# Block 1's router: the first of the largest logits found for four tiles at once

## The chip, the cores and the metric

The program runs on one core of one Trainium2 chip. All data are float32. The metric is the device time of one execution in microseconds; of several executions the median counts. The core has five engines with an instruction queue each: PE (TensorE), DVE (VectorE), ACT (ScalarE), POOL (GpSimd) and SP (SyncE, which here only issues DMAs). An engine works through its queue in order, so whatever waits holds up all that stands behind it in that queue.

## The reference

The input x has 32 sequences of 256 tokens with 128 features, 8192 tokens in all. Two blocks follow each other; each computes `x + s * silu(m)` from the layer-normalized x, where s is an attention branch and m a mixture-of-experts branch. Block 0 has two layers of softmax attention and 64 experts with eight choices per token; block 1 has linear attention and 32 experts with one choice per token. The change is in block 1's router. What it must compute, shortened:

```python
logits = x @ gate_w                        # [8192, 32]
topk_ids = jnp.argmax(logits, axis=-1)     # the first of the largest
topk_val = jnp.max(logits, axis=-1)
scores = jax.nn.sigmoid(topk_val)[:, None]
xs = x * scores
tokens_per_expert = jnp.zeros((E,), jnp.int32).at[topk_ids].add(1)
order = jnp.argsort(topk_ids)
sorted_x = xs[order]                       # rows grouped by expert, then three grouped matmuls
```

## The kernel before

A tile is 128 tokens, one per partition; a group is four tiles (512 tokens), and there are 16 groups. The kernel is written as generators that yield between steps; `run` and `rolling` interleave them. A scheduler then fixes the order of each engine's queue from the dependencies and its own estimate of times, and semaphores are set for what remains. A change in a few instructions can therefore move others on every queue.

The stages, in the order of time: block 0's attention, router and experts (to about 757 us, with the last layers' matmuls L663 and L681 reaching to 849 us); block 1's routing, interleaved with that tail and then alone (757 to 942 us); linear attention together with the scattering of rows to experts' slots (L860, 64 scatters issued by POOL, 942 to 1047 us); linear attention with the routed experts (L972, L982, L987); and the last sums.

Per group, `route` does the following, and the prediction's lines are these:

- It loads the two halves of block 0's expert sums and x by SP (L185, L187, L189), adds the halves on POOL (L188), and makes the gate on ACT and DVE (L192 to L198; the first eight groups by Tanh, the others by Silu).
- It normalizes the rows: statistics on DVE (L109, L110), four small operations on POOL (L111 to L120), the normalized rows `c_xn` on ACT (L122), four transposes on PE (L132), a copy to SBUF (L204).
- It multiplies by the router's weights (L208): four matmuls into one PSUM bank of 32 logits per tile. There are two such banks ("mm"), shared with L235, L265, L663, L681 and others.
- DVE takes, tile by tile, the eight largest logits (L216) and their places (L217, two instructions: a load of the eight values and a search); it casts the first places to float (L219) and compares the experts' numbers with them, which gives the one-hot rows `hot` (L221).
- ACT and DVE make the score from the largest logit (L223, L225); POOL scales the normalized rows with it into `s_rows` (L227).
- Running counts give each row its rank within its expert: sums on DVE (L231, L233), three matmuls (L235, L236, L239), and the rank on DVE (L240, L242, L243).

`shared1` is the shared expert of the same group: gate and up matmuls (L253, L254), activation (L256 to L260), down matmuls (L265). For groups 0 to 5 it is done later, beside the linear attention.

The work tiles come from two pools: `first_work` has one buffer per name and serves groups 0 to 3, and of the later groups those whose number is divisible by three; `mid_work` has two and serves the others. `c_xn` is such a tile, so in the small pool the next group's L122 waits until L227 of the group before has read the old rows.

When all groups are routed, the counts of all groups give the slots (`dest`, L854), and only then can the first scatter (L860) start.

Of the kernel before, what the change touches and what calls it, by code (L numbers as in the profile page):

```python
# [16 lines left out]
F32 = mybir.dt.float32  # L17
I32 = mybir.dt.int32
U32 = mybir.dt.uint32
AF = mybir.ActivationFunctionType  # L20
ALU = mybir.AluOpType
AX = mybir.AxisListType
# [3 lines left out]
P = 128  # L26
# [3 lines left out]
GT = 4  # L30
# [4 lines left out]
E1, F1 = 32, 256  # L35
# [25 lines left out]
def recurrent_kernel(ctx: ExitStack, tc: tile.TileContext, x, consts, small0, wsd, wgu, wd, small1, bias1, wr, out):  # L61
    nc = tc.nc
    vec, act, pool, pe, sp = nc.vector, nc.scalar, nc.gpsimd, nc.tensor, nc.sync

    def bcast(ap, axis, n):
        ap = ap.unsqueeze(axis)
        return ap.broadcast_to([n if i == axis else s for i, s in enumerate(ap.shape)])
# [5 lines left out]
    def bank(tag="mm", bufs=2):  # L73
        return psum.tile([P, GW], F32, tag=tag, name=f"ps_{tag}", bufs=bufs)
# [9 lines left out]
    def rows(ap, g):  # L84
        return ap[g * GW : (g + 1) * GW].rearrange("(t p) d -> p t d", p=P)
# [8 lines left out]
    def const(name):  # L94
        return con[:, cc[name][0] : cc[name][1]]
# [7 lines left out]
    def normed(wk, src, dst, on=pool):  # L103

        st = wk.tile([P, GT, 6], F32, name="bn_st")
        mv = wk.tile([P, GT, 2], F32, name="bn_mv", bufs=3)
        rs = wk.tile([P, 2, GT], F32, name="bn_rs", bufs=3)
        for j in range(GT):
            vec.bn_stats(st[:, j], src[:, j])  # L109
            vec.bn_aggr(mv[:, j], st[:, j])  # L110
        pool.tensor_scalar(rs[:, 0], mv[:, :, 1], 1.0, EPS, ALU.mult, ALU.add)  # L111
        pool.tensor_tensor(rs[:, 0], rs[:, 0], power, ALU.pow)  # L112
        if on is vec:
            ins = pool.tensor_tensor(rs[:, 1], mv[:, :, 0], rs[:, 0], ALU.mult)
            for j in range(GT):
                vec.tensor_scalar(dst[:, j], src[:, j], rs[:, 0, j : j + 1], rs[:, 1, j : j + 1], ALU.mult, ALU.subtract)
            return ins
        pool.tensor_scalar(rs[:, 1], mv[:, :, 0], -1.0, 0.0, ALU.mult, ALU.add)
        if on is act:
            pool.tensor_tensor(rs[:, 1], rs[:, 1], rs[:, 0], ALU.mult)  # L120
            for j in range(GT):
                ins = act.activation(dst[:, j], src[:, j], AF.Identity, scale=rs[:, 0, j : j + 1], bias=rs[:, 1, j : j + 1])  # L122
            return ins
        for j in range(GT):
            ins = pool.tensor_scalar(dst[:, j], src[:, j], rs[:, 1, j : j + 1], rs[:, 0, j : j + 1], ALU.add, ALU.mult)  # L125
        return ins

    def transposed(src):

        ps = bank("tr", 2)  # L130
        for j in range(GT):
            pe.transpose(ps[:, j * P : (j + 1) * P], src[:, j], ident)  # L132
        return ps
# [11 lines left out]
    at1, x_at, xt_at, hots = {}, {}, {}, {}  # L145

    def par1(name, at=0, n=None):
        a, b = s1[name]
        t, a, b = (at1["sw_c"], a - cut, b - cut) if a >= cut else (at1["sw_a"], a, b)
        return t[:, a + at : b if n is None else a + at + n]  # L150

    def room(pool_, gs):
        for g in gs:
            x_at[g] = pool_.tile([P, GT, D], F32, name=f"x_{g}")
            xt_at[g] = pool_.tile([P, GW], F32, name=f"xt_{g}")
            if g % 4 == 0:
                hots[g // 4] = pool_.tile([P, NT // 4, E1], F32, name=f"hot_{g // 4}")

    def hot_of(g):
        return hots[g // 4][:, g % 4 * GT : (g % 4 + 1) * GT]  # L160

    def begin1(pool_):
        t = at1["sw_c"] = pool_.tile([P, n_s1 - cut], F32, name="sw_c")
        sp.dma_start(t, small1[:, cut:])
        at1["rank"] = pool_.tile([P, NT], F32, name="rank")
        at1["before"] = pool_.tile([P, NG + 1, E1], F32, name="before")
        vec.memset(at1["before"][:, 0], 0.0)
        at1["ones"] = pool_.tile([P, P], F32, name="ones")
        vec.memset(at1["ones"], 1.0)
        at1["eiota"] = pool_.tile([P, E1], F32, name="eiota")  # L170
        pool.iota(at1["eiota"], [[1, E1]], base=0, channel_multiplier=0, allow_small_or_imprecise_dtypes=True)
        room(pool_, range(EARLY))

    works = []
# [1 line left out]
    def work(n):  # L176

        return works[len(works) > 1 and n % 3 > 0]

    def route(g):  # L180

        wk = works[0] if g < EARLY else work(g)
        tl = slice(g * GT, (g + 1) * GT)
        gr = wk.tile([P, GT, D], F32, tag="gate", name="c_g")
        sp.dma_start(gr, rows(moe0[0], g))  # L185
        more = wk.tile([P, GT, D], F32, tag="chan", name="c_m")
        sp.dma_start(more, rows(moe0[1], g))  # L187
        pool.tensor_tensor(gr, gr, more, ALU.add)  # L188
        sp.dma_start(x_at[g], rows(x, g))  # L189
        if g < TANH:  # L190

            act.activation(more, gr, AF.Tanh, scale=0.5)  # L192
            vec.scalar_tensor_tensor(gr, more, 1.0, gr, ALU.add, ALU.mult)
            vec.scalar_tensor_tensor(gr, gr, 0.5, s_all[:, tl], ALU.mult, ALU.mult)
        else:
            act.activation(gr, gr, AF.Silu)
            vec.tensor_tensor(gr, gr, s_all[:, tl], ALU.mult)
        vec.tensor_tensor(x_at[g], x_at[g], gr, ALU.add)  # L198
        yield
        xn = wk.tile([P, GT, D], F32, tag="tok", name="c_xn")  # L200
        normed(wk, x_at[g], xn, act)
        yield
        ps = transposed(xn)
        act.copy(xt_at[g], ps)  # L204
        yield
        lp = bank()
        for j in range(GT):
            pe.matmul(  # L208
                lp[:, j * E1 : (j + 1) * E1], xt_at[g][:, j * P : (j + 1) * P], par1("router"),
                start=True, stop=True,  # L210
            )
        lg = lp[:, : GT * E1].rearrange("p (t e) -> p t e", e=E1)
        m8 = wk.tile([P, GT, 8], F32, name="c_m8")
        i8 = wk.tile([P, GT, 8], U32, name="c_i8")
        for j in range(GT):
            vec.max(m8[:, j], lg[:, j])  # L216
            vec.max_index(i8[:, j], m8[:, j], lg[:, j])  # L217
        fi = wk.tile([P, GT], F32, name="c_fi")
        vec.tensor_copy(fi, i8[:, :, 0])  # L219
        hot = hot_of(g)  # L220
        vec.tensor_tensor(hot, bcast(at1["eiota"], 1, GT), bcast(fi, 2, E1), ALU.is_equal)  # L221
        score = wk.tile([P, GT], F32, name="c_sc")
        act.activation(score, m8[:, :, 0], AF.Tanh, scale=0.5)  # L223
        yield
        vec.tensor_scalar(score, score, 0.5, 0.5, ALU.mult, ALU.add)  # L225
        for j in range(GT):
            pool.tensor_scalar(s_all[:, g * GT + j], xn[:, j], score[:, j : j + 1], 0.0, ALU.mult, ALU.add)  # L227


        cum = wk.tile([P, GT, E1], F32, name="c_cum")  # L230
        vec.tensor_copy(cum[:, 0], hot[:, 0])  # L231
        for j in range(1, GT):
            vec.tensor_tensor(cum[:, j], cum[:, j - 1], hot[:, j], ALU.add)  # L233
        ps = bank()
        pe.matmul(ps[:, : GT * E1], const("tri"), hot.rearrange("p t e -> p (t e)"), start=True, stop=False)  # L235
        pe.matmul(  # L236
            ps[:, E1 : GT * E1], at1["ones"], cum[:, : GT - 1].rearrange("p t e -> p (t e)"), start=False, stop=True,
        )
        pe.matmul(ps[:, GT * E1 : (GT + 1) * E1], at1["ones"], cum[:, GT - 1], start=True, stop=True)  # L239
        vec.tensor_tensor(at1["before"][:, g + 1], at1["before"][:, g], ps[:, GT * E1 : (GT + 1) * E1], ALU.add)  # L240
        pos = wk.tile([P, GT, E1], F32, name="c_pos")
        vec.tensor_tensor(pos, ps[:, : GT * E1].rearrange("p (t e) -> p t e", e=E1), hot, ALU.mult)  # L242
        vec.tensor_reduce(at1["rank"][:, tl], pos, AX.X, ALU.add)  # L243
        yield
# [58 lines left out]
    def begin(g):  # L303
        yield from route(g)
        if g >= INL:
            yield from shared1(g)


    with ExitStack() as c0:
# [3 lines left out]
        wk = c0.enter_context(tc.tile_pool(name="wk0", bufs=2, side="right"))  # L313
# [489 lines left out]
    wk = ctx.enter_context(tc.tile_pool(name="wk1", bufs=2))  # L803
# [334 lines left out]
```

## Time and profile before

| | |
|---|---|
| median of three runs | 1338.09 us (1333.77 to 1339.4) |
| the profiled execution, whole | 1336.66 us |
| its span, first to last instruction | 1334.9 us |
| mean granted TensorE clock | 0.972 |
| busy: PE, PEld, DVE, ACT, POOL | 1222.2, 863.2, 943.5, 787.6, 650.6 us |
| 757 to 942 us (routing): PE, DVE, ACT, POOL busy | 156.5, 130.7, 94.3, 84.1 of 185 us |
| router on DVE: L216, L217, L219, L221 busy | 11.8, 17.3, 2.6, 4.9 us |

The span is divided by engine: an engine's busy time is the sum of its instructions' times, without waits. The granted clock is the share of full speed that TensorE was allowed[...]. A line such as "L227 <- DVE c_sc L225" in a list of waits means that the instruction of line 227 stood idle until the instruction of line 225 on DVE, which wrote c_sc, was done. In the groups of instructions the two numbers after the bar are the group's busy time and the mean time of one instruction in nanoseconds. A float32 matmul appears as two records, so "x2" of a 128x512 matmul is one instruction of the program.

### The profile page before, as it was taken

What the parts mean: (1) busy time and instruction counts of PE and PEld (TensorE: products, weight loads), DVE (VectorE), ACT (ScalarE), POOL (GpSimd) and SP (SyncE); (2) the same over time, 40 slices, a digit from 0 to 9 for tenths busy, and PEclk for the clock granted to TensorE, in tenths of its full rate; (3) what the DMA queues carried; (4) which work ended last, traced back from release to release, by engine and by line L of the source; (5) the groups of instructions that cost most, each with busy time, mean ns of one, the idle gap of its engine ahead of it and who ended that gap; (6) DMA issues with size and microseconds to landing.
All of it is one profiled execution on the core that took longest, in us unless ns stands there. A gap on an engine that the chain in (4) does not pass through costs nothing. (4 is left out here: it accounts for less than half of the span.)

```text
span 1334.9 us, 22827 instructions
## 1 busy us (share of the span) xinstructions
PE 1222.2 (92%) x7425; PEld 863.2 (65%) x7425; DVE 943.5 (71%) x3064; ACT 787.6 (59%) x1858; POOL 650.6 (49%) x1020
## 2 busy tenths in 40 slices
PE   6989999999999899999998877889999899999997
PEld 4546576566566476667666545566566688888873
DVE  4699779879879856656655766776878666676537
ACT  1786666676676567676765766444545465564543
POOL 6362822733722557656644456252477434444540
PEclk9999999999999999999999998989989899999999
DMA  6020301311211332132211133311311366767767
GB/s 183 22 56 25 112 24 48 113 31 41 96 33 40 112 76 59 34 84 56 65 20 34 36 99 94 93 49 40 113 42 45 101 206 199 220 200 220 225 218 207
DMA packets 135078, 125.80 MB, mean 94 GB/s; under 512 B 17104, under 2 KB 110256, under 8 KB 134832
## 3 DMA queue, kind: packets, MB, share of 16 engines
q1 hardware_dynamic: 123696, 108.57, 27.4%
q0 software_dynamic: 11264, 15.78, 4.9%
q8 instruction: 59, 0.97, 0.3%
q14 instruction: 59, 0.48, 0.1%
HBM read 83.63 MB, written 40.68 MB: 93 GB/s over the span
## 5 line engine op out<-in xcount | busy, mean ns | idle before, releaser
L601 ACT ACTIVATE a_pr<-ps_sc,a_nm 128x256 f32<-128x256 f32 x256 | 119.4, 480 | 58.9 <-DVE a_nm L592 58.8
L987 POOL DMA_INDIRECT back<-e_ys,e_toi x96 | 95.1, 991 | 106.3 <-ACT e_ys L986 73.2
L111 POOL TENSOR_SCALAR bn_rs<-bn_mv 128x4 f32<-128x4 f32 x112 | 27.9, 249 | 230.4 <-DVE bn_mv L110 207.0
L663 PE MATMUL ps_mm<-xt,sw 128*128 128x512 f32 x256 | 135.4, 636 | 1.6 <-ACT e_y L523 0.9
L125 POOL TENSOR_SCALAR z<-s_rows,bn_rs 128x128 f32<-128x128 f32 x256 | 129.3, 526 | 6.6
L681 PE MATMUL ps_mm<-sw,m_h 128*128 128x128 f32 x1024 | 128.3, 280 | 2.2 <-ACT e_y L523 1.3
L681 PEld LDWEIGHTS ps_mm<-sw,m_h 128*128 128x128 f32 x1024 | 119.9, 193 | 12.7 <-issue 6.0
L668 DVE SCALAR_TENSOR_TENSOR m_h<-m_h,m_z 128x512 f32<-128x512 f32 x128 | 90.4, 710 | 46.4 <-ACT m_h L667 45.9
L112 POOL TENSOR_TENSOR bn_rs<-bn_rs,power 128x4 f32<-128x4 f32 x112 | 117.4, 1048 | 1.2
L665 ACT ACTIVATE m_z<-ps_mm,fold 128x512 f32<-128x512 f32 x128 | 87.4, 686 | 30.2 <-PE ps_mm L663 29.9
L592 DVE TENSOR_REDUCE a_nm<-ps_sc 128x2 f32<-128x512 f32 x128 | 83.3, 679 | 30.6 <-PE ps_sc L586 30.5
L972 PE MATMUL ps_sc<-e_xt,e_w 128*128 128x128 f32 x768 | 100.8, 278 | 1.0 <-ACT e_xt L1009 0.6
L972 PEld LDWEIGHTS ps_sc<-e_xt,e_w 128*128 128x128 f32 x768 | 94.5, 194 | 9.8 <-issue 7.8
L586 PE MATMUL ps_sc<-a_qk,a_qk 64*128 64x256 f32 x512 | 96.4, 411 | 1.2 <-ACT a_pr L601 1.1
L524 POOL DMA_INDIRECT sums<-e_y,sidx x32 | 51.1, 1598 | 80.4 <-ACT e_y L523 42.7
L618 PE MATMUL ps_tr<-con,a_pr 128*128 128x128 f32 x512 | 76.2, 279 | 9.5 <-ACT a_pt L619 5.6
L618 PEld LDWEIGHTS ps_tr<-con,a_pr 128*128 128x128 f32 x512 | 59.5, 144 | 38.3 <-issue 20.2
L667 ACT ACTIVATE m_h<-m_z 128x512 f32<-128x512 f32 x128 | 80.8, 635 | 1.7
L860 POOL DMA_INDIRECT xslot<-s_rows,dest x64 | 68.4, 1069 | 24.1 <-issue 18.5
L619 ACT COPY a_pt<-ps_tr 128x512 f32<-128x512 f32 x128 | 71.9, 591 | 12.4 <-PE ps_tr L618 11.4
L558 PE MATMUL ps_mm<-xt,sw 128*128 128x512 f32 x128 | 70.3, 657 | 6.4 <-ACT xt L546 3.0
L627 PE MATMUL ps_mm<-a_pt,a_v 128*64 128x256 f32 x512 | 70.9, 396 | 4.2 <-ACT m_z L665 3.6
(236 smaller groups left out, 2950.4 us busy)
## 6 DMA issues: line engine op xcount, KB each, us to landing
e_w<-in_wr_dram SPq DMA_DIRECT2D x96, 384.0 KB, 4.0
xslot<-zero SPq DMA_DIRECT2D x4, 1548.0 KB, 6.7
e_x<-xslot SPq DMA_DIRECT2D x24, 258.0 KB, 3.6
e_wg<-in_wgu_dram SPq DMA_DIRECT2D x16, 384.0 KB, 3.2
x_in<-in_x_dram SPq DMA_DIRECT2D x16, 256.0 KB, 3.2
tab<-s_rows SPq DMA_DIRECT2D x16, 256.0 KB, 2.4
sums<-s_y SPq DMA_DIRECT2D x16, 256.0 KB, 2.3
sums<-zero SPq DMA_DIRECT2D x4, 1024.0 KB, 8.4
```

The lines of the kernel that those rows point to most:

```text
L112: pool.tensor_tensor(rs[:, 0], rs[:, 0], power, ALU.pow)
L125: ins = pool.tensor_scalar(dst[:, j], src[:, j], rs[:, 1, j : j + 1], rs[:, 0, j : j + 1], ALU.add, ALU.mult)
L586: pe.matmul(sc[h][:, j * SEQ : (j + 1) * SEQ], qk[0][hd, q0 : q0 + P], qk[1][hd, b * SEQ : (b + 1) * SEQ], start=True, stop=True,)
L592: vec.tensor_reduce(nm[:, 2 * h : 2 * h + 2], sc[h].rearrange("p (j k) -> p j k", k=SEQ), AX.X, ALU.max, negate=True)
L601: act.activation(pr[:, n], sc[h][:, j * SEQ : (j + 1) * SEQ], AF.Exp, bias=nm[:, n : n + 1], accum_out=su[:, n : n + 1],)
L618: pe.transpose(pts[:, n * P : (n + 1) * P], pr[:, n, k * P : (k + 1) * P], ident)
L663: pe.matmul(ps, par("w1", l * FF0 + f * P, P), xt, start=True, stop=True)
L665: act.activation(z, ps, AF.Identity, bias=fold[:, l, 3 + f : 4 + f])
L668: vec.scalar_tensor_tensor(h, h, 1.0, z, ALU.add, ALU.mult)
L681: pe.matmul(ps[:, j * D : (j + 1) * D], hs[f][:, j * P : (j + 1) * P], par("w2", l * FF0 + f * D, D), start=f == 0, stop=f == 3,)
L972: pe.matmul(ps[:, c * P : (c + 1) * P], wt[:, c * P : (c + 1) * P], xt, start=True, stop=True)
L987: ins = pool.indirect_dma_start(out=back, out_offset=bass.IndirectOffsetOnAxis(ap=to, axis=0), in_=ys, in_offset=None,)
```

## The change

The eight largest logits and their places are no longer sought. One reduction over all four tiles gives the largest logit of each token. The logits are compared with it, which marks every expert that has it; the marks are multiplied by the experts' numbers, which now run from 32 down to 1, so that the largest number among the marked is the first expert; a second reduction finds that number; and the comparison with the experts' numbers gives the one-hot rows as before. The score reads the first reduction's result. The tile `c_top` has three buffers in either pool. The lines of the kernel behind the router move by one.

```diff
         at1["eiota"] = pool_.tile([P, E1], F32, name="eiota")
-        pool.iota(at1["eiota"], [[1, E1]], base=0, channel_multiplier=0, allow_small_or_imprecise_dtypes=True)
+        pool.iota(at1["eiota"], [[-1, E1]], base=E1, channel_multiplier=0, allow_small_or_imprecise_dtypes=True)
...
         lg = lp[:, : GT * E1].rearrange("p (t e) -> p t e", e=E1)
-        m8 = wk.tile([P, GT, 8], F32, name="c_m8")
-        i8 = wk.tile([P, GT, 8], U32, name="c_i8")
-        for j in range(GT):
-            vec.max(m8[:, j], lg[:, j])
-            vec.max_index(i8[:, j], m8[:, j], lg[:, j])
-        fi = wk.tile([P, GT], F32, name="c_fi")
-        vec.tensor_copy(fi, i8[:, :, 0])
+        top = wk.tile([P, GT], F32, name="c_top", bufs=3)
+        vec.tensor_reduce(top, lg, AX.X, ALU.max)
         hot = hot_of(g)
-        vec.tensor_tensor(hot, bcast(at1["eiota"], 1, GT), bcast(fi, 2, E1), ALU.is_equal)
+        vec.tensor_tensor(hot, lg, bcast(top, 2, E1), ALU.is_equal)
+        vec.tensor_tensor(hot, hot, bcast(at1["eiota"], 1, GT), ALU.mult)
+        which = wk.tile([P, GT], F32, name="c_fi")
+        vec.tensor_reduce(which, hot, AX.X, ALU.max)
+        vec.tensor_tensor(hot, bcast(at1["eiota"], 1, GT), bcast(which, 2, E1), ALU.is_equal)
         score = wk.tile([P, GT], F32, name="c_sc")
-        act.activation(score, m8[:, :, 0], AF.Tanh, scale=0.5)
+        act.activation(score, top, AF.Tanh, scale=0.5)
```

## The prediction

> **What bounds the kernel now.** I read the page first (PE is busy 92% of the span, DVE 71%, ACT 59%, POOL 49%), then cut the span into stages, because the change touches one stage only: the routing of block 1, from the first router matmul at 757 us to the first scatter at 942 us. The stage table is the view that matters; its columns are length, busy time of PE, PEld, DVE, ACT and POOL with instruction counts, granted TensorE clock, DMA share and GB/s.
>
> ```profile
> 757.00:796.00 39.00, 34.25 (x212) 22.86 (x211) 29.37 (x110) 27.19 (x70) 19.38 (x34) 1.00 0.30 82
> 796.00:850.00 54.00, 40.15 (x230) 30.75 (x231) 35.81 (x149) 29.48 (x60) 27.80 (x45) 0.84 0.24 69
> 850.00:900.00 50.00, 41.63 (x181) 27.27 (x181) 36.41 (x205) 20.61 (x47) 26.19 (x48) 0.86 0.34 94
> 900.00:942.00 42.00, 40.49 (x240) 29.68 (x239) 29.09 (x148) 17.01 (x37) 10.72 (x29) 1.00 0.13 38
> ```
>
> In the last row PE is the bound (40.5 of 42 us). In the second and third it is not: PE idles 13.9 and 8.4 us there, and what it does runs at a granted clock of 0.84 and 0.86. No single engine is full; a chain that goes round all of them is the limit. The waits of 755 to 950 us name it (who waits, for what; total us, times, longest):
>
> ```profile
> POOL s_rows L227 <- DVE c_sc L225: 31.9, 8, 8.0
> ACT c_xn L122 <- POOL s_rows L227: 23.8, 11, 3.5
> ...
> PE ps_tr L132 <- ACT c_xn L122: 10.4, 6, 6.8
> ...
> PE ps_mm L235 <- DVE bn_mv L110: 4.2, 1, 4.2
> ...
> PE ps_mm L235 <- DVE hot L221: 2.0, 1, 2.0
> ```
>
> Read upwards from PE: it waits for normalized rows, these wait for POOL's scaling of the group before (the small work pool has one buffer of c_xn, so a new one cannot be written until the old one is scaled), and the scaling waits for the score c_sc. The fourth line says bn_mv, but the matmul's own input is hot; bn_mv merely ended last. In the timeline the worst turn of this ring looks so (start, length, engine, line; the bracket is the idle time before):
>
> ```profile
> 794.62 0.17 DVE L216 MAX8 c_m<-ps_mm 128x8 f32<-128x32 f32 x1
> 797.47 1.08 DVE L193 SCALAR_TENSOR_TENSOR c_g<-c_m,c_g 128x512 f32<-128x512 f32 x1 [2.67 <-ACT c_m L192]
> ...
> 798.64 0.14 DVE L225 TENSOR_SCALAR c_sc<-c_sc 128x4 f32<-128x4 f32 x1
> ...
> 798.89 3.22 POOL L227 TENSOR_SCALAR s_rows<-c_xn,c_sc 128x128 f32<-128x128 f32 x4 [0.90 <-DVE c_sc L225]
> ...
> 802.14 1.65 ACT L122 ACTIVATE c_xn<-x,bn_rs 128x128 f32<-128x128 f32 x4 [3.49 <-POOL s_rows L227]
> ...
> 802.69 0.86 PE L132 MATMUL ps_tr<-con,c_xn 128*128 128x128 f32 x2 [6.76 <-ACT c_xn L122]
> ```
>
> The logits were there at 792.3. The score is made from the fourth MAX8, and in DVE's fixed order the score's last step stood behind an unrelated gate operation (L193) that waited for ACT. PE stood for 6.8 us.
>
> **What the change removes and adds, per group of four tiles (16 groups).** The prices come from the groups by line and shape (busy us, mean ns):
>
> ```profile
> L217 DVE FIND_INDEX8 c_i<-c_m,ps_mm 128x8 uint32<-128x32 f32 x64 | 12.0, 188 | 0.0
> L216 DVE MAX8 c_m<-ps_mm 128x8 f32<-128x32 f32 x64 | 11.8, 184 | 18.5 <-PE ps_mm L208 18.4
> ...
> L217 DVE MATCH_VALUE_LOAD c_i<-c_m,ps_mm 128x8 f32 x64 | 5.3, 83 | 0.8
> ...
> L221 DVE TENSOR_TENSOR hot<-eiota,c_fi 128x128 f32<-128x128 f32 x16 | 4.9, 308 | 0.2
> ...
> L242 DVE TENSOR_TENSOR c_pos<-ps_mm,hot 128x128 f32<-128x128 f32 x16 | 4.5, 282 | 0.0
> L243 DVE TENSOR_REDUCE rank<-c_pos 128x4 f32<-128x128 f32 x16 | 4.4, 276 | 0.2
> ...
> L219 DVE CAST c_fi<-c_i 128x4 f32<-128x4 uint32 x16 | 2.6, 161 | 0.1
> ```
>
> - Removed: 4 x (184 + 83 + 188) + 161 = 1.98 us in 13 instructions. L221 stays.
> - Added: two reductions of 128x128 to 128x4 (276 each, the row of L243), one comparison with the logits in PSUM (282, L242: also one PSUM and one SBUF input), one product of two SBUF tiles (308, L221). Sum 1.14 us in 4 instructions. Reading PSUM in the first reduction is not shown at this size: L393 reduces 128x256 from PSUM in 419 ns, so 128 elements cannot cost more than that; I take 276 and keep 419 for the range (+2.3 us in all, on DVE).
> - Net: -0.84 us of DVE a group, -13.4 us over the stage. DVE is 70% busy there, so this is not the gain; it counts only where PE waits for DVE.
> - The reversed experts' numbers cost nothing: one iota of the same shape on POOL. No DMA is added, and none is meant to move.
>
> Three latencies change, and these count more than busy time. (1) The score needed the fourth MAX8, the tenth instruction of the old chain counting the loads, with other DVE work between the links; now it needs the first reduction. (2) The hot rows needed 14 instructions, now 5. With nothing between, 903.50 to 905.73 us is 2.2 us; five dependent operations at 0.28 us plus 0.03 us each (the step from hot to the next in that stretch) are 1.5 us. With fills between, I read from the end of L208 to the end of L221 8.1, 3.4, 5.4 and 6.3 us for the second to the fifth group. (3) The PSUM bank of the logits (two of this kind, which L663, L681, L235 and L265 share) is freed after the second instruction instead of after the last FIND_INDEX8.
>
> **Where PE gets it back**, each against the profiled execution (span 1334.9 us, whole 1336.7):
> - 796 to 802.7: in the built order the score's step on DVE now precedes L193, and on POOL one c_g addition precedes the scaling instead of two. POOL ends its norm at 795.5, + 1.27 (one L188) + 1.5 to 2.4 (four L227) + 0.5 (first c_xn): PE resumes at 799.3 to 799.7 instead of 802.7. Gain 3 us.
> - 821.0 to 825.2: hot came 5.4 us after its logits. In the new order seven short operations (statistics and the score) remain between the five links: 12 steps of about 0.2 us, 2.5 to 3 us. Gain 2.5 us, and some clock.
> - 841.7 (1.1 us idle), 863.6 (1.6; f_h L257 queued behind a FIND_INDEX8), 877.0 (2.0, hot) and 905.9 (1.0): 5.7 us in all; I take half, 2.8 us.
> - Clock. The matmuls after the pause at 821 took 4.1 us on the chain where the same shapes take 1.9 us warm (L663 0.86 a pair against 1.71): 2.2 us lost. The Trainium skill, TensorE: Matmul & The Clock Gate, "What's actually happening", says that an idle window of about 3.4 us halves the clock and a busy one restores it. By that rule shortening a pause from 4.2 to 1.5 us saves the whole 2.2 us; but 884.5 to 888 ran at half speed after a pause of only 2 us, so the row says not always. I take 2.2 us over all pauses; by the rule alone it would be about 4.
>
> Sum of gains: 3 + 2.5 + 2.8 + 2.2 = 10.5 us.
>
> **What is given back.** The stronger rule against the change is in the Trainium skill, SBUF — State Buffer, "SBUF: two separate sides": a DVE operation with two SBUF inputs and a GpSimd operation that reads SBUF exclude each other for a whole instruction. All that is removed read PSUM, and shows it: MAX8 stays within 168 to 200 ns. The new product reads two SBUF tiles. By the rule it could lose one L188 (1.27 us) a group, 20 us of DVE; the nearest row, L221, has two SBUF inputs in the same place and shows 258 to 433 ns, mean 308, 26 over its median: 16 x 0.026 = 0.4 us. I take 0.4, and keep 3 us for the range, since POOL is slowed as well (L227 370 to 992 ns).
> The second is order. The scheduler lays out every queue anew from 757 us on. On DVE the second group's "before" sum (L240), which waits for PE, now stands ahead of the next group's gate operation L193, with its add and statistics queued behind: that group's normalization comes 1 to 2 us later. On SP the loads of c_g and c_m keep their number and move by a place or two; each lands 2.9 us after issue, and a late one costs what POOL showed at 804.7 (2.6 us). I take 1.6 us for both. Next late after the score is POOL itself, busy with short pauses only from 866 to 883.
>
> Net: 10.5 - 0.4 - 1.6 = 8.5 us. Behind the stage the gain is carried over whole: the 64 scatters (L860) start only when the last group's places are known, and the order after that is nearly the old one. Profiled execution 1336.7 - 8.5 = 1328.2; the median of the three runs is 1.4 us above the profiled one, so 1338.1 - 8.5 = 1329.6, rounded 1329.5.
>
> **Rivals.**
> 1. Score early, ring unmoved. POOL's scalings come when POOL is free, not when the score is; the additions and norms of later groups fill it. For: POOL is 52% busy from 796 to 900, and the 1.95 us pause of PE at 884.5 has only POOL and ACT behind it. Against: 31.9 us of L227 waiting. Only half of the first two gaps is won: -3 us, 1335. Chance 0.27.
> 2. Slower, by order: covers are pulled out of the gaps. In the old order four gate/up matmuls of one group (L253, L254) run between the L663 at 832 to 839; in the new one none does until the last L681. They fall into the tail, where PE is full: 4 x 0.86 = 3.4 us, twice that if they meet the half clock (1.64 us each at 884). It decides if the early pauses shrink by less than these; with a late c_g load (2.6 us) on top, +6 to +9, 1345. Chance 0.20, since the new order has no new long wait in it that I can see.
> 3. The ring opens wholly: PE's idle and cold time of 796 to 900 (22 us and 16 us) falls by half: -19, 1319. Chance 0.08, within "faster".
>
> **Numbers.** My forecast 0.45 (1323 to 1333). Range 1318 to 1344: down to rival 3, up to the middle of rival 2. About 0.5% (6.7 us) is what a measurement of this kernel can tell from no change; faster than 1331.4 takes most of the forecast and all of rival 3, 0.52; within, 0.28; slower, 0.20.
>
> **What would show it.** Right: DVE's instructions of the stage about 13 us cheaper; L227 waiting for c_sc well under 31.9 us; the 6.8 and 4.2 us pauses of PE under 4 and 2; granted clock of 796 to 850 above 0.84; first scatter near 933.5 instead of 942.3. Wrong: the product at 0.5 us or more (port); the same pauses under other names, POOL first (rival 1); the last L681 earlier than 849 but the first scatter not (rival 2).

## The result and the profile after

| | before | after |
|---|---|---|
| median of six runs | 1337.19 us (1333.77 to 1339.4) | 1324.57 us (1319.01 to 1327.77) |
| ratio | | 0.990, 95% interval 0.9879 to 0.992 |
| profiled execution: span | 1334.9 us | 1324.3 us |
| PE busy, and the rest of the span | 1222.2 and 112.7 us | 1213.7 and 110.6 us |
| mean granted clock | 0.972 | 0.981 |
| last L681 (after: L682) ends | 849.3 us | 842.9 us |
| first scatter, last scatter | 942.3, 1045.4 us | 930.1, 1031.4 us |

The changed kernel is faster by 12.6 us (0.94%). In the last two sets of experiments (e9 to e12) the kernel before itself took 1352 us, 15 us more than here, so every experiment is given as a ratio to the runs of the kernel before in its own set.

The stage table again (length, busy time of PE, PEld, DVE, ACT and POOL with instruction counts, granted clock, DMA share, GB/s):

```profile
757.00:796.00 39.00, 34.32 (x211) 24.31 (x210) 28.42 (x97) 27.46 (x72) 17.75 (x31) 0.96 0.22 63
796.00:850.00 54.00, 43.61 (x249) 32.16 (x250) 40.21 (x133) 30.94 (x66) 30.61 (x52) 0.91 0.38 105
850.00:900.00 50.00, 43.37 (x232) 29.59 (x231) 36.29 (x161) 23.46 (x54) 28.41 (x56) 0.97 0.28 75
900.00:942.00 42.00, 40.69 (x206) 26.47 (x205) 30.90 (x112) 16.99 (x32) 15.24 (x25) 1.00 0.33 106
```

The second and third rows carry the difference: PE is busy 87.0 us of these 104 instead of 81.8, and at a clock of 0.91 and 0.97 instead of 0.84 and 0.86. The first row is worse than before (0.96 instead of 1.00); the second group's router matmul starts at 793.6 instead of 791.2. The last row holds the first scatters already.

The waits of 755 to 940 us (who waits, for what; total us, times, longest):

```profile
POOL s_rows L228 <- DVE c_sc L226: 36.3, 11, 7.0
ACT c_xn L122 <- POOL bn_rs L120: 20.2, 8, 3.8
...
ACT c_xn L122 <- POOL s_rows L228: 8.7, 5, 2.3
...
PE ps_tr L132 <- ACT c_xn L122: 5.6, 5, 2.7
...
PE ps_mm L236 <- DVE bn_mv L110: 1.5, 1, 1.5
```

PE's wait for c_xn fell from 10.4 to 5.6 us and ACT's wait for the scaling from 23.8 to 8.7. POOL's own wait for the score did not fall: 36.3 instead of 31.9 us. ACT now waits for POOL's norms (L120) instead. The turn of the ring that took PE 6.8 us looks so in the timeline:

```profile
793.62 1.08 PE L208 MATMUL ps_mm<-sw_c,xt 128*128 128x32 f32 x8
...
794.74 0.29 DVE L216 TENSOR_REDUCE c_top<-ps_mm 128x4 f32<-128x128 f32 x1 [0.86 <-PE ps_mm L208]
794.94 0.68 DVE L669 SCALAR_TENSOR_TENSOR m_h<-m_h,m_z 128x512 f32<-128x512 f32 x1
795.54 0.28 DVE L218 TENSOR_TENSOR hot<-ps_mm,c_top 128x128 f32<-128x128 f32 x1
795.74 0.23 DVE L226 TENSOR_SCALAR c_sc<-c_sc 128x4 f32<-128x4 f32 x1
...
799.19 1.42 POOL L228 TENSOR_SCALAR s_rows<-c_xn,c_sc 128x128 f32<-128x128 f32 x4
...
801.20 0.48 PE L132 MATMUL ps_tr<-con,c_xn 128*128 128x128 f32 x1 [2.69 <-ACT c_xn L122]
```

The score's last step (L226) starts 2.1 us after the first router matmul (7.4 before), POOL does not wait for it here, and the pause is 2.69 us. Two more things can be read: the last reader of the logits' PSUM bank (L218) is done 2.2 us after the bank was taken, where the old chain's last FIND_INDEX8 was done after 7.5 us at this place; and L216 is listed with 0.29 us, yet the next instruction starts 0.20 us after it. Listed durations of DVE overlap. The new router operations, from the groups of instructions (busy us, mean ns):

```profile
L216 DVE TENSOR_REDUCE c_top<-ps_mm 128x4 f32<-128x128 f32 x16 | 4.6, 289 | 15.2 <-PE ps_mm L208 15.0
...
L218 DVE TENSOR_TENSOR hot<-ps_mm,c_top 128x128 f32<-128x128 f32 x16 | 4.5, 283 | 0.1
...
L219 DVE TENSOR_TENSOR hot<-hot,eiota 128x128 f32<-128x128 f32 x16 | 4.5, 281 | 0.0
L221 DVE TENSOR_REDUCE c_fi<-hot 128x4 f32<-128x128 f32 x16 | 4.4, 275 | 0.1
```

### The profile page after: what moved, and what is told of

Read it like the earlier page. It is cut to its first block, busy times and chain, and to the rows that moved or that the text cites. A ratio compares the mean times of both kernels' runs of the same rounds, so it can differ in the third digit from the quotient of the medians.

```text
span 1324.3 us, 22686 instructions
## 1 busy us (share of the span) xinstructions
PE 1213.7 (92%) x7425; PEld 857.2 (65%) x7425; DVE 937.6 (71%) x2920; ACT 786.5 (59%) x1858; POOL 647.8 (49%) x1020
## 5 line engine op out<-in xcount | busy, mean ns | idle before, releaser
L664 PE MATMUL ps_mm<-xt,sw 128*128 128x512 f32 x256 | 133.8, 629 | 2.6 <-ACT m_z L666 1.3
L682 PE MATMUL ps_mm<-sw,m_h 128*128 128x128 f32 x1024 | 130.0, 283 | 2.3 <-ACT e_y L524 1.3
L682 PEld LDWEIGHTS ps_mm<-sw,m_h 128*128 128x128 f32 x1024 | 121.9, 196 | 12.9 <-issue 5.8
L666 ACT ACTIVATE m_z<-ps_mm,fold 128x512 f32<-128x512 f32 x128 | 87.4, 686 | 28.3 <-PE ps_mm L664 27.5
L559 PE MATMUL ps_mm<-xt,sw 128*128 128x512 f32 x128 | 68.9, 644 | 6.3 <-ACT xt L547 3.0
```

The costliest lines, as they stand in the source:

```text
L664: pe.matmul(ps, par("w1", l * FF0 + f * P, P), xt, start=True, stop=True)
L666: act.activation(z, ps, AF.Identity, bias=fold[:, l, 3 + f : 4 + f])
L682: pe.matmul(ps[:, j * D : (j + 1) * D], hs[f][:, j * P : (j + 1) * P], par("w2", l * FF0 + f * D, D), start=f == 0, stop=f == 3,)
```

## The experiments

The theories at the start: A, the early score opens the ring (the prediction's main step); B, the short chain to the one-hot rows and DVE's lighter load; C, the chance of another order in the queues. B was then split into H (length of the chain), W (DVE's work) and the hold of the PSUM bank. "Hold" below is the mean over 16 groups, from the start of the group's first router matmul to the end of the last instruction that reads its logits in PSUM, read from the timelines. The last three columns come from one profiled execution each, which need not be typical: it took 11.5 us less than the median in e10, and 4 to 6 us more in e2, e4 and e8.

| kernel | ratio to before (95%) | hold, us | first scatter, us | PE busy, rest of span, us |
|---|---|---|---|---|
| before | 1 | 4.67 | 942.3 | 1222.2, 112.7 |
| e1 early score | 1.0013 (0.9999 to 1.0027) | 4.84 | 942.5 | 1222.6, 111.9 |
| e7 ring opened before | 0.9991 (0.998 to 1.0003) | 4.44 | 938.4 | 1221.7, 107.5 |
| e8 bank held | 0.9996 (0.9984 to 1.0009) | 4.98 | 940.6 | 1229.4, 108.0 |
| e2 late score | 0.9957 (0.9937 to 0.9977) | 2.19 | 938.0 | 1223.1, 110.1 |
| e3 padded | 0.9929 (0.9903 to 0.9955) | 2.11 | 934.6 | 1220.9, 107.5 |
| e9 bank freed before | 0.9918 (0.9889 to 0.9948) | 1.47 | 934.6 | 1224.6, 109.7 |
| e6 score control | 0.9905 (0.9881 to 0.9929) | 2.18 | 928.1 | 1214.7, 104.3 |
| after | 0.990 (0.9879 to 0.992) | 2.16 | 930.1 | 1213.7, 110.6 |
| e5 no tie, padded | 0.9883 (0.9861 to 0.9905) | 2.17 | 928.5 | 1212.7, 107.9 |
| e4 no tie | 0.9824 (0.9799 to 0.9848) | 2.03 | 915.6 | 1218.9, 99.0 |
| e10 other banks, before | 0.997 (0.9955 to 0.9986) | 5.64, in sc | 935.1 | 1218.9, 115.7 |
| e11 other banks, after | 0.9877 (0.9845 to 0.9909) | 2.27, in sc | 925.2 | 1222.6, 108.4 |
| e12 no tie, other banks | 0.9874 (0.9848 to 0.9901) | 2.22, in sc | 919.4 | 1222.1, 112.0 |

**e1, the early score alone.**

```diff
         i8 = wk.tile([P, GT, 8], U32, name="c_i8")
+        top = wk.tile([P, GT], F32, name="c_top", bufs=3)
+        vec.tensor_reduce(top, lg, AX.X, ALU.max)
...
-        act.activation(score, m8[:, :, 0], AF.Tanh, scale=0.5)
+        act.activation(score, top, AF.Tanh, scale=0.5)
```

> The kernel before, with one reduction per group added (128x128 to 128x4) from which only the score is made; the one-hot rows still come from the eight largest and their places. DVE gets 16 x 0.28 = 4.5 us more work. Theory A (the gain comes from the early score, which lets POOL scale and frees c_xn): the PE pauses at 802 and its successors shrink as in the changed kernel, 1328 to 1332 us, first scatter near 936. Theory B (the gain comes from the short chain to the one-hot rows and from less DVE work): no gain, 1336 to 1340. Theory C (the gain is mostly the chance of another order in the queues): anything between 1325 and 1342, with pauses in new places.

Measured: 1.0013, no gain. ACT's wait for the scaling fell as the prediction had it, from 23.8 to 13.4 us, and still PE waited longer for c_xn (10.4 before):

```profile
PE ps_tr L132 <- ACT c_xn L122: 15.0, 8, 4.1
ACT c_xn L122 <- POOL s_rows L229: 13.4, 11, 2.2
```

The last of block 0's tail came 3.7 us sooner (845.6), and all of that was lost between there and the first scatter. Theory A does not stand by itself.

**e2 and e6, the late score and its control.** Both add the same operation; only what tanh reads differs.

```diff
+        late = wk.tile([P, GT], F32, name="c_late", bufs=3)
+        vec.scalar_tensor_tensor(late, which, 0.0, top, ALU.mult, ALU.add)
-        act.activation(score, top, AF.Tanh, scale=0.5)      # e6 keeps this line
+        act.activation(score, late, AF.Tanh, scale=0.5)     # e2
```

> The changed kernel, but the score's tanh reads a copy of the largest logit that also depends on c_fi, the second reduction, so that the score comes only when the one-hot rows are nearly made (one 128x4 operation more per group, about 0.16 us). The rest of the change stays. Theory A: most of the gain is lost, 1331 to 1336 us, and ACT's L122 waits for POOL's scaling by 20 us or more again. Theory B: the gain stays, 1324 to 1328. Theory C: between 1320 and 1337 with no tie to the score.

> The control to the late score: the changed kernel with the same extra 128x4 operation per group (it depends on c_fi and writes a copy of the largest logit), but the score is read from the first reduction as in the changed kernel, and nothing reads the copy. The two have nearly the same order on PE. If the late score cost its 6 us by being late: 1324 to 1327 us here. If it was the chance of the order that the extra operation brought: 1329 to 1332.

Measured: 0.9957 with the score late, 0.9905 with the same operation and the score early. So the lateness costs some 0.5%, 7 us, and the order that the extra operation brought costs nothing that can be seen. But the sign expected for e2, ACT waiting 20 us or more for the scaling, did not come: that wait was 13.4 us in e2 and 8.2 in e6. An early score is worth about half of the gain here, and nothing in e1, where the rest of the old chain stood: something else came first.

**e3 and e5, DVE's time given back, and e4, a shorter chain.** e4 takes the product, the second reduction and the last comparison out; e3 adds the padding to the changed kernel and e5 adds it to e4.

```diff
-        vec.tensor_tensor(hot, hot, bcast(at1["eiota"], 1, GT), ALU.mult)          # e4, e5
-        which = wk.tile([P, GT], F32, name="c_fi")
-        vec.tensor_reduce(which, hot, AX.X, ALU.max)
-        vec.tensor_tensor(hot, bcast(at1["eiota"], 1, GT), bcast(which, 2, E1), ALU.is_equal)
+        junk = wk.tile([P, GT], F32, name="c_junk")                                # e3, e5
+        for j in range(3):
+            vec.tensor_reduce(junk, hot, AX.X, ALU.max)
```

> The changed kernel with three idle reductions of the one-hot rows per group (128x128 to 128x4, 0.28 us each, 13.4 us in all), which give DVE back the time that the change took from it; nothing reads them. Theory A and the prediction (DVE's busy time is not the gain): within 2 us of the changed kernel, 1323 to 1327 us. Theory B: half of the 13.4 us or more comes back, 1331 to 1338. Theory C: 1320 to 1334.

> The changed kernel without the product, the second reduction and the last comparison: the one-hot rows are the comparison of the logits with their maximum. What it leaves out is the choice of the first among equal logits; without equal logits the rows are the same. Three of five DVE operations go, 16 x 0.85 = 13.6 us, and the one-hot rows come 0.9 us earlier. Theory A: the score is as early as before, so little is gained, 1321 to 1324 us. Theory B: as much again as the change brought, 1312 to 1318. Theory C: 1315 to 1332.

> The kernel without the choice of the first among equal logits (two operations from logits to one-hot rows) plus the three idle reductions per group of the padded kernel, 13.4 us of DVE, placed behind the one-hot rows. DVE has as much to do as in the changed kernel; only the chain to the one-hot rows is shorter, by three operations (0.85 us). Theory H (the length of that chain counts): it keeps most of the shorter kernel's gain, 1314 to 1318 us. Theory W (DVE's work counts): it is back at the changed kernel, 1322 to 1326. Theory C (chance of the order): anywhere from 1312 to 1330.

Measured: padding costs 0.29% on the changed kernel (3.9 us; the intervals overlap) and 0.59% on e4 (7.9 us; they do not). e4 gains another 0.76%, which padding takes back for the larger part. So padding is not free, about 6 us in the mean for 13.4 us of listed time. But it is not only work: 18 of the 48 reductions in e3 and 25 in e5 stand ahead of the running counts in DVE's order. Counted from the start of the router matmul, the counts are ready after 6.9 us in e3 and 5.8 in e5, against 6.2 in the changed kernel and 4.6 in e4 (means of 16 groups). In e5 the one-hot rows come after 2.2 us instead of 4.3, and its ratio is 0.17% below the changed kernel's, with overlapping intervals: the chain to the rows by itself brings nothing clear. The chain on to the counts and DVE's work changed together in e3, e4 and e5, and these runs do not separate them. In e4 PE is at its limit just before the first scatter, 39.2 of 39.6 us at full clock:

```profile
876.00:915.60 39.60, 39.21 (x214) 27.46 (x214) 25.22 (x107) 17.54 (x38) 12.13 (x32) 1.00 0.13 39
```

**e7, the ring opened in the kernel before.**

```diff
-        xn = wk.tile([P, GT, D], F32, tag="tok", name="c_xn")
+        xn = wk.tile([P, GT, D], F32, tag="out" if g in (1, 3) else "tok", name="c_xn")
```

> The kernel before with a second buffer for c_xn in groups 1 to 3 (odd groups take the tile of the name out, which no group uses at that time), so that ACT's L122 no longer waits for POOL's scaling of the group before; the order of PE changes little (34 of 1306 rows). The prediction's first step (the 6.8 us pause shrinks and this is carried over whole): 1331 to 1334 us, with the pause under 4 us. If that pause is only the first of several in parallel, as the early score alone suggests: 1335 to 1338, with the time given back at a later pause.

Measured: 0.9991. The 6.8 us pause is gone from the place of the c_xn transposes, and the next thing that PE needs is late instead, the one-hot rows (PE's timeline):

```profile
795.31 1.06 PE L132 MATMUL ps_tr<-con,c_xn 128*128 128x128 f32 x4
800.54 0.77 PE L235 MATMUL ps_mm<-hot,con 128*128 128x128 f32 x2 [4.17 <-DVE hot L221]
```

Of the pauses that the prediction added up, this one by itself was worth about 1 us (by the interval, less than 3).

**e8 and e9, the PSUM bank.** e8 makes the changed kernel hold the logits' bank until the one-hot rows are made. e9 makes the kernel before let it go after one copy; the old search then runs on the copy.

```diff
+        held = wk.tile([P, GT, E1], F32, name="c_cum")      # e8, behind the last comparison
+        vec.tensor_tensor(held, lg, hot, ALU.mult)
...
+        keep_lg = hot_of(g)                                 # e9, ahead of the eight largest
+        vec.tensor_copy(keep_lg, lg)
+        lg = keep_lg
```

> The changed kernel with one product of the logits and the finished one-hot rows per group (read by nothing, 0.28 us, 4.5 us in all), which keeps the logits' PSUM bank until the one-hot rows are made, as the kernel before did. If the early release of the bank is part of the gain: 1328 to 1332 us, with PE waiting at ps_mm for DVE. If not, only the 4.5 us of DVE work count at the rate of the padded kernel (3.2 of 13.4 us): 1324.5 to 1327.

> The kernel before, with one copy per group of the logits from PSUM into the tile of the one-hot rows (128x128, about 0.28 us, 4.5 us of DVE in all); the eight largest and their places are sought in the copy. All of the old chain stays, and it starts 0.3 us later; but the PSUM bank is free after the copy instead of after the last search. Theory B (the bank: it was held 5.1 us a group in the kernel before, 2.2 us in the changed one, from the start of the first router matmul to the last reader): 6 to 11 us under the kernel before, hold near 2 us. Rival (the chain to the one-hot rows and the score have to be short, the bank matters only through them): 0 to 4 us above the kernel before.

Measured: e8 loses the whole gain (0.9996), although its score (3.1 us in the mean after the start of the router matmul, 3.0 in the changed kernel) is as early and its one-hot rows (4.3 in both) come as soon; its running counts come 0.7 us later, as they do in e3, which keeps most of its gain. The product is written into the buffers of the running counts, but that does not explain the loss: the matmuls that read those buffers before it (L242) had ended at least 4.4 us earlier in every group. e9 wins most of the gain (0.9918), although the old search is all there, with the score made from it, and DVE has an instruction more per group. Its score and its rows did come 0.9 us sooner in the mean than in the kernel before (4.3 and 4.9 us instead of 5.2 and 5.9), so the bank is not all that changed; but e1, with the score at 3.0 us, and e8, with the rows at 4.3, gained nothing. The two runs cross. With the logits in the two banks, the kernels with a mean hold of 4.4 to 5.0 us (before, e1, e7, e8) do not differ clearly, and the seven with 1.5 to 2.2 us all gain, 0.4 to 1.8%. Theory C, the chance of another order, is not ruled out for any single run, but it would have to fall the same way in all of them. In e8's timeline of DVE the bank's last reader is L224, 1.8 us behind the comparison L218 that ended the hold in the changed kernel (the router matmul started at 792.27):

```profile
794.19 0.29 DVE L218 TENSOR_TENSOR hot<-ps_mm,c_top 128x128 f32<-128x128 f32 x1
...
795.98 0.29 DVE L224 TENSOR_TENSOR c_cum<-ps_mm,hot 128x128 f32<-128x128 f32 x1
```

And e9's PE timeline shows another order. The copy (DVE) is done 1.4 us after the bank was taken, and the rows' matmul L238 and then the tail's L684, which needs one of the same two banks, run ahead of the c_xn transposes, where the kernel before has its 6.8 us pause; yet the score's last step starts only 5.5 us after the router matmul (7.4 in the kernel before, 2.1 in the changed one). That the free bank allowed this order is inferred:

```profile
794.12 1.08 PE L208 MATMUL ps_mm<-sw_c,xt 128*128 128x32 f32 x8
...
795.24 0.29 DVE L214 COPY hot<-ps_mm 128x128 f32<-128x128 f32 x1 [0.86 <-PE ps_mm L208]
...
799.63 0.17 DVE L228 TENSOR_SCALAR c_sc<-c_sc 128x4 f32<-128x4 f32 x1 [1.87 <-ACT c_sc L226]
...
800.36 0.76 PE L238 MATMUL ps_mm<-hot,con 128*128 128x128 f32 x2 [1.50 <-DVE hot L224]
800.92 1.06 PE L684 MATMUL ps_mm<-sw,m_h 128*128 128x128 f32 x4
803.38 0.48 PE L132 MATMUL ps_tr<-con,c_xn 128*128 128x128 f32 x1 [1.40 <-ACT c_xn L122]
```

**e10 to e12, the logits in another bank.** The logits' bank is taken from the four of the gate and up matmuls, in the kernel before, the changed one and e4.

```diff
-        lp = bank()
+        lp = bank("sc", 4)
```

> The kernel before, with the logits in one of the four banks of the gate and up matmuls (sc) instead of one of the two that L235, L265, L663 and L681 share (mm). No instruction is added. Theory B: the two banks are no longer held by the old chain, 5 to 11 us under the kernel before; what could eat it is that gate and up matmuls or block 0's tail then wait for their banks. Rival (chain): within 2 us of the kernel before.

> The changed kernel with the logits in one of the four sc banks in the same way. Theory B: the bank is held only 2.2 us by then, so that little is left: 0 to 4 us under the changed kernel, 10 to 16 under the kernel before. If the two banks are still the limit of the stage, more than 5 us under the changed kernel.

> The kernel without the choice of the first among equal logits (this is what it leaves out), with the logits in one of the four sc banks as well: the two steps that gave most, together. If what they give adds up (1.8% and 0.2 to 0.3%): 2.0 to 2.2% under the kernel before. If the stage's limit is elsewhere by then (PE was busy 98% of the last 40 us before the first scatter in the kernel without the choice): 1.6 to 1.9% under it, no better than without the other banks.

Measured: 0.997, 0.9877 and 0.9874. In the kernel before it brings 0.3%, 4 us, less than the 5 expected at least and less than half of e9: the old chain now holds one of four banks that the shared expert needs, for 5.6 us in the mean, and still delays the score and the one-hot rows. In the changed kernel 0.2% is within the intervals: the hold was short already. e12 is no better than e11 and seems worse than e4, but was not timed beside it. One reason may be a pause shortly behind the first scatter: at 939.15 us PE has stood 4.62 us ahead of sc matmuls of the linear attention (L892), behind a late activation (f_h, L257), in a place where e4 has no pause that long.

The fastest of all is e4, 0.9824; with the choice of the first among equals, e11, the changed kernel and e6 are the fastest, and the runs do not tell them apart.

## Why the prediction was right, and where it was not

The direction, the size (8.5 us expected, 12.6 measured) and the range hold. The steps do not all, and that the sum came near is partly luck. In the profiled executions, which differ by 10.6 us, less idle time of PE over the whole span gave 2.1 us, where the terms for the pauses less what is given back make 6.3; less busy time gave 8.5, where the term for the clock makes 2.2. The two errors have opposite signs.

- **The pauses:** 6.76 became 2.69 us (a gain of 3 was expected, 4.1 came), 4.19 became 1.53 (2.5 expected, 2.7 came). PE's idle time from 757 us to the first scatter fell from 28.5 to 22.1 us, 6.4; the prediction's three terms made 8.3.
- **Clock, the mis-sized term.** 2.2 us were expected. Both kernels have the same 7425 PE instructions, and their busy time fell by 8.5 us; of the 10.6 us by which the span shrank, only 2.1 are idle time. At (1 - clock) x length, 12.1 us of full clock were regained over the span: 8.5 up to the first scatter (6.8 of these from 757 us on), 5.1 from there to 1080 us (0.94 before, 0.98 after), which the prediction did not look at, and 1.5 lost behind that. Over all executions the median clock was 0.972 for the kernel before (31 and 43 runs of the first two sets) and 0.9805 for the changed one (six runs), so the profile does not stand alone. The clock is not in every gain: e3 gains 0.7% at a median clock of 0.973. e8 shows it in the other direction: its profiled span is 13.1 us longer than the changed kernel's, and PE is not idle for longer but busy for 15.7 us more. The rule of the Trainium skill that was weighed there (TensorE: Matmul & The Clock Gate, "What's actually happening": an idle window of about 3.4 us halves the clock) would have given 4; with pauses of at most 2.7 us the stage from 796 to 850 us still ran at 0.91, so shorter pauses cost clock as well. At 871 to 875 us, right behind a pause of 1.29 us, the changed kernel's clock was 0.57.
- **The ring, the step whose reason failed.** The pause was credited to the score alone, and its shortening to the whole kernel. In e8 the score is early and the pause is as short as in the changed kernel, and the gain is gone:

```profile
799.82 0.48 PE L132 MATMUL ps_tr<-con,c_xn 128*128 128x128 f32 x1 [2.68 <-ACT c_xn L122]
```

Score without bank (e1) brings nothing either, and the ring opened without both (e7) about 1 us; bank without early score (e9) brings 0.8%, and with the bank free, a late score costs 0.5% (e2 against e6). The early release of the bank was named as the third latency and then given no price; it had the largest, and the score has one only beside it. The waits of the kernel before could not show it: no row of PE's waits names L217, the bank's last reader. The trace of e6 has one such row (PE ps_mm L666 <- DVE hot L218, 0.7 us once), that of e4 one of 0.9 us. The likely reason is that the scheduler puts a matmul that needs the bank later in the queue, and PE then waits for something else; how much of the cost arises so, and how much by waiting on the chip, the runs don't separate. (The expectation of e9 gives the old hold as 5.1 us; that runs to the start of the cast behind the last search, and to the end of the last search it is 4.7.)
- **DVE.** The operations removed cost 31.7 us by their listed durations and those added 18.0, so 13.7 less, as expected. But listed durations overlap: DVE's busy time fell by 5.9 us only, and the 48 idle reductions of e3 (13.4 us listed) raised it by 7.8. That DVE's time is "not the gain" may be wrong in part: padding cost 4 us in e3 and 8 in e5, though some of this comes from where the padding stands.
- **The sign of POOL's wait was wrong.** L228's wait for c_sc rose to 36.3 us in the faster kernel, and is 38 to 44 in e1, e6, e8 and e9: a wait of an engine with time to spare. The wait of ACT for the scaling was the one to watch in the two kernels, but e2 and e1 show that it doesn't measure the gain either.
- **Given back.** The port cost was looked for in the wrong instruction. The product took 281 ns in the mean, below L221's 308, but none of the sixteen met an L188 on POOL. Six other DVE operations did from 757 to 942 us, and were held until L188 ended, 5.0 us in all beyond their medians; in the kernel before it was two, 1.3 us. This is the exclusion that the prediction weighed. (It also has all that was removed reading PSUM; the cast L219 reads SBUF.) So DVE lost 3.7 us more where 0.4 was put down. One of them is a running count, otherwise 0.18 us, and the counts' matmul waited for it:

```profile
821.18 1.27 POOL L188 TENSOR_TENSOR c_g<-c_g,c_m 128x512 f32<-128x512 f32 x1
821.44 1.06 DVE L234 TENSOR_TENSOR c_cum<-c_cum,hot 128x32 f32<-128x32 f32 x1
...
822.79 0.46 PE L237 MATMUL ps_mm<-c_cum,ones 128*128 128x96 f32 x2 [0.35 <-DVE c_cum L234]
```

What this cost the kernel was not measured; e4 has eleven such cases and is the fastest. The order cost is visible, DVE standing 4.38 us at L241 ahead of L193 (at 803.63 us); it was not measured by itself. Not foreseen: a new 1.95 us pause at 769 us and a clock of 0.96 in the first row; the second group's router matmul comes 2.4 us later.
- **Carried over whole?** The first scatter came 12.2 us sooner (8.7 expected), the last one 14.0, the end 10.6. From the last scatter to the end the changed kernel takes 292.9 us instead of 289.5. e6, with nearly the same routing, takes 287.7, so this is no necessary price; where it comes from was not tried.
- **Rivals.** The deferred gate and up matmuls of rival 2 did not decide: the tail from the last L682 to the first scatter is 87.2 us instead of 93.0. Rival 1 (ring unmoved, POOL next) describes e1 better than the changed kernel. Rival 3 came nearer than its chance of 0.08: of its 19 us in the stretch from 796 to 900, cold time gave 8.5 (15.4 to 6.8, more than half) and idle time 5.2 (22.2 to 17.0, less than half).

## What to carry to other kernels

When a change shortens the time for which a shared PSUM bank is read, give that a price of its own: sum the hold from the matmul that takes the bank to its last reader over all uses, and ask what else stands in line for the same banks. One copy out of PSUM per group tests it in either direction. Where a list of waits names one producer, another may be as late behind it (e7): undo the wait alone before crediting it with the pause. And a pause that has become short is not yet time won (e8): look at the clock and at the next pause too.

## What the runs showed of the hardware

Consecutive DVE instructions overlap in the profile: 48 reductions of 128x128, 0.28 us each by their rows, added 0.16 us each to DVE's busy time. A reduction of 128x128 from PSUM took 289 ns, from SBUF 275, a comparison with one input in PSUM 283: no difference that matters at this size. A matmul record of 128x512 took 592 ns at full clock and up to 1061 at half (L253 before the change).

A DVE operation that reads two SBUF tiles and begins while POOL adds two (L188, 1.27 us) ends with or just after that addition: running counts of 0.18 us took 1.18 and 1.06 us, and the gate's L194, otherwise 0.68, took 1.76 and ended 0.55 us behind L188. The score's last step, a 128x4 operation with one tile input, was held in the same way (0.17 to 1.03 us), and these few cases are why its mean rose from 162 to 267 ns and L194's from 689 to 808; the medians did not move. Operations that read PSUM, and the statistics (L109), kept their times beside L188 (L218 0.28 us, L109 0.28). The reverse occurs too: in the kernel before, an L188 that began beside L194 on DVE is listed with 3.04 us, while DVE's operations kept their times. The product of two SBUF tiles met only shorter operations of POOL and took 251 to 322 ns.
